# All transfers of the samples issued by SyncE, matrices over h and k and the inverse's scratch in 128 rows, a plan that knows of eight transfers under way

## The chip, the core and the metric

The kernel runs on one core of one Trainium2 chip. A core has five engines that run their own instruction streams: TensorE (PE; its weight loads are listed apart as PEld), VectorE (DVE), ScalarE (ACT), GpSimd (POOL) and SyncE (SP). Transfers between DRAM and the on-chip memory are carried by 16 DMA engines; they are issued by SP or by ACT, each with a queue of its own. The metric is the device time of one execution in microseconds; shorter is better.

## The reference, cut to what matters

The input x has 32 images of 56 x 56 pixels and 96 channels. Two layers follow one another.

```python
# layer 0: a convolution block whose weights are mixed per image (E = 4 experts, M = 384)
pooled = mean(x, axis=(1, 2)); rw = sigmoid(pooled @ Wr + br)
Wk = einsum('be,ecm->bcm', rw, Wpw)
h = relu(bn1(einsum('bhwc,bcm->bhwm', x, Wk) + rw @ bpw))
h = relu(bn2(sum over e of (depthwise 3x3 of h with Wdw[e] + bdw[e]) * rw[:, e]))
Wk2 = einsum('be,emf->bmf', rw, Wpwl)
x = bn3(einsum('bhwm,bmf->bhwf', h, Wk2) + rw @ bpwl) + x

# layer 1a: tokens t [32, 3136, 96]; a product in the frequency domain, hidden width 192
h = relu(bn1(layernorm(t) @ w1.T))
X = fft(h, axis=1, norm='ortho')
xr = relu(X.real * rd - X.imag * id + rb); xi = relu(X.imag * rd + X.real * id + ib)
t = t + bn2(ifft(xr + 1j * xi, axis=1, norm='ortho').real @ w2.T)

# layer 1b: a feed-forward net whose operands are rounded to an 8-bit and a 16-bit float
t = t + qlinear(relu(qlinear(layernorm(t), W1, b1)), W2, b2)
```

The Fourier transform over 3136 tokens is split in two steps of 56 (3136 = 56 x 56): one along the image's h with a twiddle factor, one along w. The values before the transform are real, so 29 of 56 frequencies suffice (K1).

## The kernel before, in words

**An image at a time, but in one long plan.** `record(b)` writes down the operations of image b: for each its engine, a duration, a due time, what it reads, writes and which buffers it takes. Nothing is issued then. When all 32 images are recorded, `Plan.order()` plays the operations through with the durations it was given, engine by engine, and the order in which they start there is the order in which the instructions are issued (lines 1445 to 1448). Each engine then runs its own instructions strictly in that order. The due times come from `WANT` (offsets from the image's start at multiples of `period`) and from `NUDGE`, one number for each operation of an image, added to its due time (line 233). An operation of DVE or ACT that reads the PSUM banks is due `HURRY` earlier. An operation that has been ready for `PATIENCE` and lacks a buffer holds that buffer back from operations behind it (line 319).

**Transfers in the plan.** `move` (line 225) adds a transfer: an operation of SP, or of ACT with `by="ACT"`, that takes 0.35 or 0.475 us to issue; its data then arrive one transfer after the other, `DMA_LAG` after the issue at the earliest. `slack` (2.0 for most, 0.0 for those by ACT) is added to the time at which its data are counted as ready to send.

**Layer 0** is done for two halves of the image and three chunks of 128 of the 384 channels. Chunk 2 goes by `by_vector` (line 845), where DVE makes eight of nine taps of the depthwise filter. Chunks 0 and 1 go by `by_tensor` (line 904), where TensorE does the filter. There the expand matmuls (32 columns at a time, `ps<-x,wk 97*32`) leave pixels of four parities on four groups of 32 partitions; ACT copies them with a ReLU into `hg`, and four transfers spread them into `hp` so that channel group and parity are on the right partitions ("hp<-h" in the profile, line 941). TensorE convolves, ACT brings the result back into `hp`, and four transfers send it into `hid` ("h<-hp", line 978), from where `project` multiplies it into 96 channels. Both sets of four are issued by ACT: 2 halves x 2 chunks x 8 = 32 transfers an image.

**Layer 1a** is done in four strips of 14 columns of the image. `da` (line 1101) is the matrix along h for the strip, loaded from the DRAM scratch `dad` by two transfers of 56 rows each, one for each parity of w. The result goes through the DRAM scratch `gd` ("gd<-g", "g<-gd"), the frequencies are handled in seven groups, and the inverse's first step goes into the DRAM scratch `yd` ("yd<-y", line 1302). For the inverse's second step `yt` (from `yd`) and `dd` (the matrix over k, from the input `dftd`) are loaded for each strip; both have 116 rows, and each is loaded by one transfer of 112 rows and one of 4 (lines 1319 and 1326). `back_h` multiplies them.

**Layer 1b** follows for the strip on TensorE, ACT, DVE and POOL, and the result leaves by SP ("out_dram<-xs").

**Preparation.** Before the images, constants are loaded and combined. `pack` (line 521) brings the matrix along h into the two halves' layout and writes it to `dad`, of 112 rows.

Of the kernel before, what the change touches and what calls it, by code (L numbers as in the profile page):

```python
# [19 lines left out]
C = 96  # L20
# [134 lines left out]

DMA_LAG = 1.9


def packets(n, size):
# [7 lines left out]
WANT = dict(period=120.0, expand=0.0, vector=1.4, forward=10.7, forward_step=27.0, freq=172.2,  # L167
            freq_step=7.0, tail=259.2, tail_step=26.5, x=17.0, mix=33.5, project=33.0)

HURRY = 160.2  # L170

PATIENCE = 0.2
# [4 lines left out]
    12.4, 22.1, 10.5, 25.3, -46.9, 6.9, 9.8, -31.8, 17.7, 22.8, 16.9, -1.6, 25.2, -10.2, -27.6, 5.2, 14.6, -15.7,  # L177
    49.7, 34.1, 32, 57.2, 7.6, -16.6, -19.8, -22.6, -16.6, -11.1, -12.4, -12.2, -15.8, 11.6, 14.1, 13.8, 29.2, 15,
    3.4, -6.4, 6.1, -32.1, -24.8, 30.6, 37.1, 14.9, 25.7, 0.1, -8.5, -2.7, -25.9, -54.5, -54.2, 12.1, 29.2, -31.5,
    14.5, 5.3, 2.9, -1, -2.8, -4.9, 18.2, 26.7, 23, 3.3, 18.2, -4.4, 7.7, 4.5, -11.1, -7.5, -11, -1.7,  # L180
    -46.2, -17.3, -2.1, -23.9, 13.1, -8.7, 14.3, -11, 14.7, 25.3, 3.9, 5.6, 0.7, 2.5, -16.3, -15, -2.1, 7.5,
    -10.9, 9.9, -11.5, -28.5, 0, 1.6, 10.1, -10.4, 11, 16.7, 28.4, 0.7, -37.6, -9.4, -13.9, -7.1, -28.9, -6.9,
    -14.8, -27.7, 0.8, 28.3, 20.5, 10.5, -1.8, 10.5, 18.1, -29.6, -37.7, -27.2, 25.5, 4.7, 14.8, 25.1, 12.5, 10.2,
    20.6, -6.3, -50.8, -56.5, 10, 27.5, 8.1, -9.8, -9.2, 20.2, -4.7, -2.5, 35.8, 15, 38.3, -1.6, 5.8, 15.5,
    11.1, -0.9, -2.7, -3.3, -3.5, -23.1, -10.1, -46.5, -6.8, 5.4, -14.9, -8.6, -6.9, -32.5, -11.2, 10.7, 14.5, 13.5,
    20.5, 16.8, -3.3, 10.4, 31.9, 2.9, 17, 4.1, -3.4, -17.3, -2.5, 12.5, 20.1, -8.8, 14.4, 11.1, 14.5, 1.9,
    -1.6, 19.4, 0.8, 10.7, -33.2, -38.3, -2.5, -4.1, -3, 11.9, -5.4, -47.3, 26.7, 14, -1, -16, -0.6, -29.3,
    8.7, 1.3, 11.8, -0.5, 0.5, 9.4, -37.9, -30.9, 1.7, -9.6, -1.5, 7.4, 9.9, -38.9, 21, 10.9, 10.2, -1.8,
    -12.2, -40.3, 13, 29.1, -5.1, 5.8, -4.9, -13.3, -42.9, -49.7, -55.1, -20.4, -40.3, -2.6, -34.5, -54.1, 4.9, -23.7,
    -7.1, -18.3, -6, -40.4, 19.5, 14.4, -3.4, -2.3, 13.7, 6.4, -29, -29.1, -17.7, -24.8, -15.7, -2.8, -2.9, -26.4,  # L190
    12.5, 9.1, -7.2, -12.2, -23, -49.8, 2.1, -10.6, -58.6, -12.9, -26.5, -2.4, -15.2, 14.5, -37.7, -10, -37.3, -0.7,
    -10.9, 4, -24.3, -12.2, 1.7, 5.4, -28.2, -2.2, -37, -17.2, -12.4, -6.4, 20.8, -17.2, -39, 42, -50.4, 5.6,
    3.6, -3.9, 29.1, 5.9, -27.6, 9.4, -25.9, 5, 13.4, 5.9, -10.2, 11.5, 28.1, 20.5, -24.7, 5.4, -47.4, 7.1,
    4.1, -0.7, 11.5, 2, -73.8, 33.8, -38.8, -14.4, 3.6, 2.1, 23.7, 20.1, -18.2, -7.7, -41.5, 24.5, -1.4, 2.2,
    -5.1, 1.1, 18.4, 19.6, -9.6, -15.1, -41.3, -12.8, 0.4, -1.1, 48.3, 4.2, -51.5, 58.4, -59.6, 3.4, -3.1, 0.8,
    16.9, 25.7, -5.4, 5, -24.6, 11.5, 10.5, 1.9, 0.7, 7.3, 9.9, 17.5, -1.7, 13.1, -14.5, 2, -7.2, -3.5,
    28.9, -11.4, -53.9, 49.3, -50.2, -1.7, -1, -1, 11, 8.9, -35, -5.1, -46.9, -12.2, -2.5, -0.3, -21.2, -2.3,
    -5.5, -6.3, -26.8, 9.4, -33.7, 9.5, 1.9, 2.6, 5.1, -2.1, -53.9, 51.5, -45.3, -2.6, 0, -9.3, 9.9, -4,
    -31.7, 3.9, -37.4, -7.8, 2.4, 11.4, -7.7, -4, 2, 14.8, -33.6, -3.7, -23.7, 6.6, 1.7, 0.9, 28.6, -8.6,
    -44.6, 46.4, -32.1, -9.4, 18.6, 0.4, -0.7, 8.6, -30, 2.9, -24.1, -6.2, -4.7, 14.1, -14, 4.8, 11.2, 9.1,  # L200
    -48.8, 3.6, -31.8, 12.2, -7.4, -10.5, 35.7, -7.9, -25, 41, -12.1, 1.4, 25.3, 3.5, 27.6, 2.1, 30.6, -6,
    3.2, 1.4, 22.5, 45.6, 14.3, -40, -4.7, 24.9, -15.7, 78.9, -13.2, 34.9, 1.3, 44.8, -2, 26.3, -29.2, 74.9,
    -3.3, 17.2, 8.9, 0.3, 1.1, 18.7, 25.2, 11.9, 28.4, 18.6, 8.5, 13.8, 8.9, 40.3, 2.5, -1, 2.9, 1.6,
    28.9, -11.8, -69.5, -27, 6.7, -13, 76.4, -12.9, 15.7, -4, 88.9, -6, 4.1, -21.6, 57.2, -1.6, 3.2, 0.6,
    3, -16.1, -4.9, 15.1, -11.5, 16.1, 5.5, 1.6, 9, 4.3, 28.2, 4.6, 27.2, 4.9, 3.5, 16.5, -10.6, -30.1,
    -22.7, 22.8, -15, 63.3, -5.2, 29.1, -11.2, 62.8, -40, -2.3, -15.3, 62.2, -13.6, -48, -20.5, -22, -39.8, -14,
    -12.2, -13, -2.6, 5.9, 33.1, 8.9, 9.1, 43.2, -29.5, 9.5, -8, -9.9, 17.9, -14.4, -50.3, -36.4, 39.3, 18.7,
    78.8, -12.6, 25.5, -2.1, 81.9, 3.6, 10.8, -8.5, 76.4, 8.5, 37.6, 21.8, 17, 24.2, 6, 21.7,
# [4 lines left out]
class Plan:  # L213
# [49 lines left out]
    def order(self):  # L263
# [5 lines left out]
        until = {"DVE": 0.0, "POOL": 0.0}  # L269
        waiting = []  # L270
        done = []

        def push(t, kind, x):
            nonlocal n
            n += 1
            heapq.heappush(events, (t, n, kind, x))
# [5 lines left out]
        def start(op, now):  # L282
            for b in op.takes:
                b.got = b.ring.take(b.n)
            begin = now
            if op.port:
                if op.eng == "POOL" and until["DVE"] > now:
                    waiting.append(op)
                    free["POOL"] = float("inf")
                    done.append(op)  # L290
                    return
                begin = max(now, until["POOL"])
                until[op.eng] = begin + op.dur
            op.end = begin + op.dur
            free[op.eng] = op.end
            done.append(op)
            if op.size:
                nonlocal moved
                moved = max(moved, op.end + DMA_LAG) + op.size
                push(moved, "end", op)  # L300
            else:
                push(op.end, "end", op)
# [73 lines left out]
def kernel(  # L376
# [97 lines left out]
    dad = dram.tile([PB, NQ, 2 * KR], F32, tag="dad", name="dad")  # L474

    with tc.tile_pool(name="prep", bufs=1) as pp:
        def temp(shape, name, dt=F32):
# [9 lines left out]
            par[:, :], ident[:, 0:PB].rearrange("z (p h) -> z p h", p=2), AX.X, ALU.add  # L487
# [29 lines left out]
        big = temp([PB, NQ // 2, PA], "big")  # L517
        small_a = temp([PB, NQ // 2, 2 * KR], "small_a")
        nc.vector.memset(small_a, 0.0)

        def pack(i):
            nc.scalar.dma_start(big, dfta[:, i * (NQ // 2) : (i + 1) * (NQ // 2)])
            v = big.rearrange("z q (k p r) -> z q k p r", p=2, r=2)
            to = small_a.rearrange("z q (r k) -> z q k r", r=2)[:, :, 0:K1]
            for q in range(NQ // 2):
                nc.vector.tensor_scalar_mul(to[:, q], v[:, q, :, 0], par[:PB, 0:1])
                nc.vector.scalar_tensor_tensor(to[:, q], v[:, q, :, 1], par[:PB, 1:2], to[:, q], ALU.mult, ALU.add)
            nc.sync.dma_start(dad[:, i * (NQ // 2) : (i + 1) * (NQ // 2)], small_a)
# [137 lines left out]
        for i in range(2):  # L666
            pack(i)
        nc.vector.tensor_copy(fw1, f1, saturate=False)
# [26 lines left out]
    r_dd = places(2, [PA, SQ, PB], F32, "dd")  # L695
# [9 lines left out]
    r_yt = places(2, [PA, SQ, C], F32, "yt")  # L705
# [11 lines left out]
    r_yd = ring(2, [PA, NQ, C], F32, "yd", dram)  # L717
# [25 lines left out]
    def record(b):  # L743
# [160 lines left out]
        def by_tensor(h, c, due, hid):  # L904
# [36 lines left out]
            for r in range(4):  # L941
                move(
                    packets(32, 6960), due - WANT["expand"] + 2,
                    lambda r=r: se.dma_start(
                        hp.ap[32 * r : 32 * r + 32].rearrange("p g n -> p (g n)"), hg.ap[r::4, :]
                    ),
                    by="ACT", slack=0.0,
# [30 lines left out]
            for q in range(4):  # L978
                move(
                    packets(32, 6272), due + 3,  # L980
                    lambda q=q: se.dma_start(
# [3 lines left out]
                    by="ACT", slack=0.0,  # L985
# [98 lines left out]
        for st in range(NS):  # L1084
# [17 lines left out]
            for p in range(2):  # L1102
                move(
                    packets(S, 1792), due - 5,
                    lambda p=p, st=st, da=da: sy.dma_start(
                        da.ap[XW * p : XW * p + S], dad[S * p : S * p + S, st * SQ : st * SQ + SQ, :]
                    ),
                    writes=[(da, p)], takes=[da] if p == 0 else [],
                )
            for q0, nq in ((0, 4), (4, 3)):  # L1110
# [27 lines left out]
                def along_h(q0=q0, nq=nq, ps=ps, ha=ha, da=da):  # L1138
# [11 lines left out]
                    "PE", 0.78, due + 3, along_h, reads=[(ha, 0), (da, 0), (da, 1)], writes=[(ps, 0)], takes=[ps, g],  # L1150
# [160 lines left out]
        for st in range(NS):  # L1311
# [7 lines left out]
            for a, z in ((0, PB), (PB, PA)):  # L1319
                move(  # L1320
                    packets(z - a, 2688), due - 6,
                    lambda a=a, z=z, st=st, yt=yt: sy.dma_start(yt.ap[a:z], yd.ap[a:z, st * SQ : st * SQ + SQ, :]),
                    reads=[(yd, i) for i in range(len(GROUPS))], writes=[(yt, a)], takes=[yt] if a == 0 else [],
                )
            dd = Buf(r_dd)
            for a, z in ((0, PB), (PB, PA)):
                move(
                    packets(z - a, 3136), due - 6,
                    lambda a=a, z=z, st=st, dd=dd: sy.dma_start(dd.ap[a:z], dftd[a:z, st * SQ : st * SQ + SQ, :]),
                    writes=[(dd, a)], takes=[dd] if a == 0 else [],  # L1330
                )
            ps = Buf(banks, 2)

            def back_h(ps=ps, yt=yt, dd=dd):
                for q in range(SQ):
                    te.matmul(
                        ps.pair[:C, 128 * q : 128 * q + 128].rearrange("c (p h) -> c p h", h=64)[:, :, 0:S],
                        yt.ap[:, q, :],
                        dd.ap[:, q, :].rearrange("c (p h) -> c p h", h=S),
# [223 lines left out]
```

## Time and profile before

| what | value |
|---|---|
| median of the runs | 4509.07 us (3 runs, 4507.47 to 4515.27) |
| the profiled execution's own time | 4500.26 us |
| its span, first to last instruction | 4498.5 us |
| mean granted TensorE clock | 0.955 |
| PE, DVE, ACT, POOL busy | 4036.7, 3514.9, 2518.6, 1484.5 us |
| transfers issued by ACT in the images | 512 hp<-h, 512 h<-hp |
| moved by all queues | 719.51 MB, 160 GB/s |

How to read the profile: times are microseconds unless marked ns. A group of instructions is named by line, engine, operation and out<-in in the program's own names, buffer numbers left out; after the bar stand its busy time, the mean of one, and the idle time of its engine just before such instructions, with what ended that idle time. Nearly every operation is issued through one helper, so its line is L370 everywhere and groups are told apart by tiles. A row of waits reads: who waited, for whom, the total, how many times, the longest. "SPq" and "ACTq" are the instructions that issue transfers; they are not counted as busy, nor is the time in which an engine stands before one. A wait for several semaphores is put down to the one that came last. A granted clock of 0.50 means that TensorE ran at half speed.

### The profile page before, as it was taken

Reading aid. Unit: us, or ns where it says so; the run is one execution under the profiler, and the core shown is the slowest. Engines: PE = TensorE matmul, PEld = TensorE weight load, DVE = VectorE, ACT = ScalarE, POOL = GpSimd, SP = SyncE. Lnnn points to the kernel's source line nnn. Section 1 sums busy time; section 2 is a strip of 40 time slices with the busy share of each in tenths; the row PEclk is TensorE's granted clock in tenths of the full one; section 3 lists DMA queues with packets and bytes.
Section 4 is the critical chain, followed back from the end, with each engine's and each line's share of the span. In section 5 each row is a group of like instructions: output and inputs, shape, how many; then the busy total and the mean of one; then the engine's idle time right before and its main releaser. Section 6 shows DMA issues by size and latency. Waiting matters only on the chain. (4 is left out here: it accounts for less than half of the span.)

```text
span 4498.5 us, 114325 instructions
## 1 busy us (share of the span) xinstructions
PE 4036.7 (90%) x44802; PEld 2547.7 (57%) x44802; DVE 3514.9 (78%) x9663; ACT 2518.6 (56%) x4982; POOL 1484.5 (33%) x1361
## 2 busy tenths in 40 slices
PE   2999999999999999999999999999999999989896
PEld 1455555556555555555565655565555556555564
DVE  5677878888877787877878778888878888877765
ACT  2455655565665555655566655565655565665453
POOL 1123333333333333333333333333333333333333
PEclk9999999999999999999999999999999999999987
DMA  4866677676677676676666676766677676677652
GB/s 100 158 149 161 153 184 173 164 173 159 161 164 173 161 163 157 156 181 161 162 157 156 160 182 169 169 168 158 161 183 172 164 169 160 156 171 167 154 140 71
DMA packets 436660, 719.51 MB, mean 160 GB/s; under 512 B 160954, under 2 KB 294522, under 8 KB 436122
## 3 DMA queue, kind: packets, MB, share of 16 engines
q1 hardware_dynamic: 382176, 492.72, 43.2%
q10 hardware_dynamic: 53946, 219.49, 23.6%
q8 instruction: 354, 5.80, 0.6%
q14 instruction: 184, 1.51, 0.1%
HBM read 286.14 MB, written 209.06 MB: 110 GB/s over the span
## 5 line engine op out<-in xcount | busy, mean ns | idle before, releaser
L370 DVE SCALAR_TENSOR_TENSOR h<-h,small,h 128x784 f32<-128x784 f32 x1024 | 1094.7, 1072 | 89.1 <-ACT h L370 64.8
L370 POOL CAST h<-h 128x784 fp8e5<-128x784 f16 x384 | 454.3, 1194 | 1184.4 <-DVE h L370 1184.4
L370 PE MATMUL ps<-x,wk 97*32 97x435 f32 (+2 forms) x4608 | 715.2, 600 | 125.0 <-ACT h L370 86.2
L370 ACT ACTIVATE h<-ps 128x435 f32<-128x435 f32 (+2 forms) x768 | 394.2, 531 | 304.1 <-PE ps L370 231.4
L370 PE MATMUL ps<-hp,wg 32*32 32x392 f32 x16384 | 503.8, 511 | 23.6 <-issue 19.4
L370 PE MATMUL ps<-dftb_s,g 112*128 112x112 f32 (+1 forms) x3776 | 424.0, 281 | 69.0 <-DVE tmpa L370 33.6
L370 PEld LDWEIGHTS ps<-x,wk 97*32 97x32 f32 (+1 forms) x4608 | 197.4, 121 | 453.7 <-ACT h L370 218.4
L370 ACT ACTIVATE hp<-ps,small 128x392 f32<-128x392 f32 x512 | 262.9, 589 | 308.9 <-PE ps L370 202.8
L370 POOL TENSOR_TENSOR ln<-ln,mhalf 120x7 f32<-120x7 f32 (+1 forms) x256 | 420.6, 1643 | 21.3
L370 PEld LDWEIGHTS ps<-dftb_s,g 112*128 112x128 f32 (+1 forms) x3776 | 335.0, 165 | 162.0 <-DVE tmpa L370 51.9
L370 DVE SCALAR_TENSOR_TENSOR ha<-ps,ln,nshift 120x192 f32<-120x192 f32 x896 | 308.6, 409 | 143.8 <-PE ps L370 135.0
L370 ACT ACTIVATE h<-h 128x784 f32<-128x784 f32 x128 | 109.6, 856 | 554.8 <-DVE h L370 233.2
L370 PE MATMUL ps<-h,wk 32*96 32x392 f32 x4096 | 413.7, 540 | 3.7 <-DMA h<-hp 3.6
L370 PEld LDWEIGHTS ps<-hp,wg 32*32 32x32 f32 x16384 | 286.7, 104 | 181.9 <-issue 93.1
L370 DVE BATCH_NORM_STATS2 ln<-ps 120x6 f32<-120x96 f32 (+1 forms) x1792 | 318.4, 248 | 72.5 <-PE ps L370 72.2
L370 PE MATMUL ps<-w1c,x 96*120 96x192 f32 x1792 | 345.9, 337 | 3.8 <-ACT hp L370 2.4
L370 ACT CAST h<-ps 128x784 f16<-128x784 f32 x384 | 299.2, 814 | 85.3 <-PE ps L370 62.0
L370 DVE TENSOR_SCALAR nt<-ps,ln 112x96 fp8e5<-112x96 f32 x896 | 267.0, 368 | 97.8 <-POOL ln L370 96.7
L370 PEld LDWEIGHTS ps<-h,wk 32*96 32x96 f32 x4096 | 212.1, 176 | 229.1 <-issue 108.2
L370 POOL TENSOR_TENSOR xs<-xs,y 96x784 f32<-96x784 f32 x128 | 214.0, 1671 | 353.5 <-ACT tmpb L370 199.1
L370 PEld LDWEIGHTS ps<-w1c,x 96*120 96x120 f32 x1792 | 290.4, 185 | 59.2 <-issue 25.1
L370 POOL COPY park<-x 96x784 f32<-96x784 f32 x128 | 109.9, 859 | 600.2 <-DVE x L370 574.2
(171 smaller groups left out, 7083.9 us busy)
## 6 DMA issues: line engine op xcount, KB each, us to landing
hp<-h ACTq DMA_DIRECT2D x512, 217.5 KB
h<-hp ACTq DMA_DIRECT2D x512, 196.0 KB
gd<-g SPq DMA_DIRECT2D x384, 192.0 KB
g<-gd SPq DMA_DIRECT2D x192, 336.0 KB
dd<-in_dftd_dram SPq DMA_DIRECT2D x128, 343.0 KB
xd<-park SPq DMA_DIRECT2D x128, 294.0 KB
xs<-xd SPq DMA_DIRECT2D x128, 294.0 KB
yt<-yd SPq DMA_DIRECT2D x128, 294.0 KB
```

What stands on the lines that cost most here:

```text
L370: return self.tc.keep_in_program_order(method(*args, **kwargs))
```

## The change

**Who issues.** The eight transfers of `by_tensor` (four hp<-h, four h<-hp) are issued by SP instead of ACT, at the same due times and with the same slack of 0.0. ACT issues none in the images any more.

**128 rows.** `dad` gets 128 rows, with each parity's 56 rows at rows 0 and 64 and zeros between, so `da` comes by one transfer of 128 rows instead of two of 56. `yd` gets 128 rows, and a copy of `dftd` with 128 rows, `ddd`, is made in DRAM during the preparation, with the rows past 116 zero; `yt` and `dd` come by one transfer of 128 rows instead of two of 112 and 4. `back_h` still multiplies the first 116 rows. That is twelve transfers an image less. In the preparation `big` and `small_a` are cleared by POOL, `big` is loaded by two transfers a half, and `rows_of_128` issues five transfers on ACT.

**The plan.** `order()` now keeps eight lanes: a transfer begins when the first of them is free again, and gives one back when its data have arrived. `NUDGE` has new values throughout (562 numbers for 574, one for each operation of an image), `HURRY` goes from 160.2 to 115.8, `PATIENCE` from 0.2 to 0.0 and `period` from 120.0 to 120.2. The order of the instructions on every engine follows from these.

```diff
+LANES = 8
...
-HURRY = 160.2
-PATIENCE = 0.2
+HURRY = 115.8
+PATIENCE = 0.0
...
         until = {"DVE": 0.0, "POOL": 0.0}
+        lanes = [0.0] * LANES
...
+            if op.size:
+                begin = max(now, lanes.pop(0))
             op.end = begin + op.dur
...
                 moved = max(moved, op.end + DMA_LAG) + op.size
+                lanes.append(moved + LAG["SP"])
...
-    dad = dram.tile([PB, NQ, 2 * KR], F32, tag="dad", name="dad")
+    dad = dram.tile([128, NQ, 2 * KR], F32, tag="dad", name="dad")
+    ddd = dram.tile([128, NQ, PB], F32, tag="ddd", name="ddd")
+    r_yd = ring(2, [128, NQ, C], F32, "yd", dram)
...
-        nc.vector.memset(small_a, 0.0)
+        nc.gpsimd.memset(big, 0.0)
+        nc.gpsimd.memset(small_a, 0.0)
...
-            nc.scalar.dma_start(big, dfta[:, i * (NQ // 2) : (i + 1) * (NQ // 2)])
+            part = slice(i * (NQ // 2), (i + 1) * (NQ // 2))
+            for p in range(2):
+                nc.scalar.dma_start(big[XW * p : XW * p + S], dfta[S * p : S * p + S, part])
...
+        def rows_of_128():
+            zero = temp([128 - PA, NQ, PB], "zero")
+            nc.gpsimd.memset(zero, 0.0)
+            nc.scalar.dma_start(ddd[0:PB], dftd[0:PB])
+            nc.scalar.dma_start(ddd[PB:PA], dftd[PB:PA])
+            nc.scalar.dma_start(ddd[PA:128], zero)
+            for t in r_yd.places:
+                nc.scalar.dma_start(t[PA:128], zero[:, :, 0:C])
...
-                    lambda r=r: se.dma_start(
+                    lambda r=r: sy.dma_start(
                         hp.ap[32 * r : 32 * r + 32].rearrange("p g n -> p (g n)"), hg.ap[r::4, :]
                     ),
-                    by="ACT", slack=0.0,
+                    slack=0.0,
...
-                    lambda q=q: se.dma_start(
+                    lambda q=q: sy.dma_start(
...
-                    by="ACT", slack=0.0,
+                    slack=0.0,
...
-            for p in range(2):
-                move(
-                    packets(S, 1792), due - 5,
-                    lambda p=p, st=st, da=da: sy.dma_start(
-                        da.ap[XW * p : XW * p + S], dad[S * p : S * p + S, st * SQ : st * SQ + SQ, :]
-                    ),
-                    writes=[(da, p)], takes=[da] if p == 0 else [],
-                )
+            move(
+                packets(128, 1792), due - 5,
+                lambda st=st, da=da: sy.dma_start(da.ap, dad[:, st * SQ : st * SQ + SQ, :]),
+                writes=[(da, 0)], takes=[da],
+            )
...
-            for a, z in ((0, PB), (PB, PA)):
-                move(
-                    packets(z - a, 3136), due - 6,
-                    lambda a=a, z=z, st=st, dd=dd: sy.dma_start(dd.ap[a:z], dftd[a:z, st * SQ : st * SQ + SQ, :]),
-                    writes=[(dd, a)], takes=[dd] if a == 0 else [],
-                )
+            move(
+                packets(128, 3136), due - 6,
+                lambda st=st, dd=dd: sy.dma_start(dd.ap, ddd[:, st * SQ : st * SQ + SQ, :]),
+                writes=[(dd, 0)], takes=[dd],
+            )
```

`yt` changes in the same way as `dd`, and reads `yd`.

## The prediction, made before the result was known

> **What bounds the kernel.** I read the first part of the page, then the steady stretch by window, then who ended TensorE's idle time there, then ACT's and SP's timelines at the gaps.
>
> ```profile
> PE 4036.7 (90%) x44802; PEld 2547.7 (57%) x44802; DVE 3514.9 (78%) x9663; ACT 2518.6 (56%) x4982; POOL 1484.5 (33%) x1361
> q1 hardware_dynamic: 382176, 492.72, 43.2%
> q10 hardware_dynamic: 53946, 219.49, 23.6%
> ```
>
> TensorE is the bound: 90% busy, nothing else over 78%. q1 is SP's queue, q10 ACT's; together they keep the 16 DMA engines two thirds busy. One image recurs in the trace every 135.07 us: from 337.7 to 4254.6 us are 29 images. The windows of that stretch, of one undisturbed image, and of three pieces of it (columns: window, its length, busy time of PE, PEld, DVE, ACT, POOL, granted clock, DMA share, GB/s):
>
> ```profile
> 3040.80:3047.60 6.80, 6.46 (x33) 2.13 (x37) 4.57 (x11) 3.42 (x7) 4.45 (x3) 0.50 1.01 234
> 3047.60:3173.90 126.30, 117.24 (x1371) 75.80 (x1363) 104.17 (x288) 75.25 (x150) 42.46 (x40) 1.00 0.68 165
> 3173.90:3180.70 6.80, 6.72 (x33) 2.12 (x37) 4.53 (x11) 3.16 (x7) 4.14 (x3) 0.50 1.00 214
> 337.70:4254.60 3916.90, 3615.10 (x40602) 2281.83 (x40606) 3141.60 (x8613) 2275.06 (x4494) 1347.92 (x1218) 0.97 0.70 165
> 3041.10:3174.00 132.90, 123.72 (x1404) 77.95 (x1404) 108.55 (x298) 78.48 (x156) 46.72 (x43) 0.98 0.70 168
> ```
>
> In 3916.9 us TensorE idles 301.8. It also runs at half clock for 6.8 us once an image, at one place (3040.8, 3173.9). The trace's clock marks give 269.7 us of half clock in this stretch, 41 pieces; half of it, 135 us, is lost. Idle time and lost clock, 437 us, are all that faster surroundings can give back here: 15 us an image. TensorE's waits in the same stretch (total, times, longest):
>
> ```profile
> PE ps L370 <- ACT h L370: 114.9, 62, 4.2
> PE ps L370 <- DVE tmpa L370: 74.4, 108, 1.2
> PE ps L370 <- issue: 29.3, 20, 4.1
> PE ps L370 <- ACT g L370: 27.4, 23, 2.6
> PE ps L370 <- ACT n L370: 26.4, 29, 0.9
> PE ps L370 <- ACT hp L370: 7.5, 10, 2.4
> ```
>
> ACT ends 176 us of it. Of "ACT h", 86.2 us stand before one form, the 97x32 expand matmuls, in gaps of 2.3 to 4.2 us, one an image. The timelines at one of them, ACT's then TensorE's:
>
> ```profile
> 3034.49 1.14 ACTq L370 DMA_DIRECT2D hp<-h  x2
> 3038.64 1.12 ACTq L370 DMA_DIRECT2D hp<-h  x2
> 3039.81 0.86 ACT L370 ACTIVATE h<-h 128x784 f32<-128x784 f32 x1 [3.19 <-DVE ln L370]
> 3041.14 1.68 PE L370 MATMUL ps<-x,wk 97*32 97x435 f32 x8 [2.44 <-ACT h L370]
> ```
>
> ACT finishes its Cast at 3036.6, stands until 3038.6 before it may issue two more transfers, spends 1.12 us on them, and only then reads the banks that TensorE waits for. The half clock begins in this gap. What ACT stood for is plainer at 2196, ACT's rows and then TensorE's:
>
> ```profile
> 2196.42 6.55 ACTq L370 DMA_DIRECT2D h<-hp  x4
> 2203.09 1.54 ACT L370 ACTIVATE hp<-ps,small 128x392 f32<-128x392 f32 x3 [5.92 <-DMA dd<-in_dftd_dram]
> 2206.12 1.46 PE L370 MATMUL ps<-hp,wg 32*32 32x392 f32 x2 [4.09 <-issue]
> ```
>
> h and hp have nothing to do with dd. The trace shows why: all 3477 transfers of both queues carry one of eight completion semaphores, 434 or 435 each, and a transfer waits for the one that had its semaphore before. So ACT stands for SP's transfers.
>
> **The change, part by part.** Per image, 75 transfers are issued by SP and 32 by ACT, 107 over eight semaphores. The three merges (da, yt, dd) take 12 from SP and the move adds 32: 95, all SP's.
>
> *ACT freed.* 32 issues at a median of 0.475 to 0.49 us are 15.5 us an image, and the waits before them (324 us in the run by the trace's gaps, 10 an image) go too. ACT is 56% busy, so this counts only where TensorE waits behind it. The recurring gap is that: **-86 us**. The irregular gaps of the kind at 2206 ("issue" at the hp,wg form 12.7 here, "ACT g" 27.4, "ACT hp" 7.5; 48 us) I take for half: **-24 us**, since g is copied beside the issues but also late by its own inputs.
>
> *The clock.* The Trainium skill, TensorE: Matmul & The Clock Gate, "Why this matters for your kernels", warns of idle gaps over about 3 us and of one idle window. By that rule a 2.4 us gap costs 2.4 us and no clock, and this term is nothing. The row says otherwise: half clock begins at gaps of 2.44 and 2.52 us, while the 1.2 us gaps before DVE tmpa show none. The measurement decides: 29 pieces belong to the recurring gap, 6.6 us each, halved, 96 us; all 41 are 135. In the other order of work another gap can be long enough, so I take half of 135: **-67 us**. By the rule the sum below would be 67 us slower.
>
> *SP lengthened.* Before: gd 16 at 0.60, da 8 at 0.54, 51 others at about 0.33, 31 us an image. After: 16 at 0.60, 4 at 0.54, 43 at 0.33, 32 at 0.48, about 41 us of 135. There is room, but SP works in order, and its waits are long:
>
> ```profile
> SPq L370 <- ACT y L370: 762.6, 199, 8.8
> SPq L370 <- POOL park L370: 526.4, 111, 11.1
> ```
>
> That is 3.8 and 4.7 us a time, for yd<-y and xd<-park. A set of hp<-h or h<-hp behind one is late, and behind it the conv or projection matmuls. Now TensorE waits almost never for them; from the last landing of a set of hp<-h to its conv are 1.9 us in the lowest quarter of the 128 sets, 4.7 in the middle. On the other side the four issues of a set, spread over 4.7 us on ACT (median), can go in 2. The cost lies between 0 and 256 us (each of 256 sets late by 1 us); I take a quarter of the sets late by 1 us, the lowest quarter: **+64 us**. The Trainium skill, DMA: Bandwidth & Descriptors, "Issuing engines are not separate DMA queues", calls the sequencer time saved "usually small relative to the DMA itself"; by it the ACT term is nothing and this one stays, 4564. The row of 2.0 + 1.12 us inside a 2.44 us gap speaks against it here.
>
> *More rows, fewer transfers.* 128 rows for 112 or 116 add 28 KB to da, 31.5 to yt, 36.8 to dd a strip, 12.3 MB on 719.5: DMA share 0.70 becomes 0.71. The wait for this stays under the transfers' slack (yt's landing is 7 us ahead of its matmul in the lowest quarter); nothing. If it were not hidden, 1.7% of 3000 busy DMA us would be 51.
>
> *Preparation.* One memset moves from DVE to POOL and two are new; x's 1920 columns took 1.65 us there, so big's 1624 and zero's 3136 take about 4 us together, early, while POOL idles until 82 us. ACT gets seven more issues before image 0: two for the second halves of big, five for ddd and the pads. The 1.4 MB copy of dftd into ddd is 9 us at 160 GB/s. SP's first dd load, at 74 us, must wait for it, and behind that stand image 1's first x loads and wk2's pieces. Between 0 and 20; **+5 us**.
>
> *Order.* NUDGE, HURRY, PATIENCE and the lane count give every engine another order. The trace of before can't show it; its bound is the 437 us above on one side and as much again on the other. I leave the middle at nothing and widen the range.
>
> **Sum**, against the profiled execution's own 4500.3 us (span 4498.5): -86 -24 -67 +64 +5 = -108, 4392. The median of the runs shown, 4509.1, is 9 us above that execution, so **4401**; the measurement's own spread makes about 0.2% (9 us) the least that can be told from no change.
>
> **Rivals.**
> (a) ACT freed entirely and nothing in return: all of 86 + 48 + 135 = 269 less, 4231 and 9: 4240. For it: TensorE's own work at full clock is (3615 - 135) / 29 = 120 us an image, and no other engine is near that. Against: DVE at 78% ends 74 us of waits that the change does not touch, and SP's price.
> (b) SP's queue holds the sets (slower). Place: hp<-h and h<-hp behind yd<-y and xd<-park. If 4 us are added before every set, the slack above leaves a mean of 1 us late; 256 sets are 256 us, such stalls keep the half clock, and only 110 of the gain stays: 4500 - 110 + 256 + 5, and 9: 4660. It decides from about 0.7 us a set (177 / 256). For it: SP's waits; against it: twelve fewer transfers an image over the eight semaphores, and room on SP.
> (c) The stall changes its owner: the recurring gap goes, another of over 2 us comes with its half clock, and the irregular gaps stay; 4500 - 86 + 64 + 5, and 9: 4492, 0.4% faster, with "same" inside its spread.
> (d) The move hides: the gaps follow from data, not from issue, no change, 4509. Against it is the row at 2196.
>
> **Chances.** Sum as above 0.50 (own range 4320 to 4475), (a) 0.15, (c) 0.12, (d) 0.03, (b) 0.20. Faster: 0.50 + 0.15 + two thirds of (c) = 0.73; same 0.04 of (c) and 0.02 of (d): 0.06; slower 0.21. The range leaves out two fifths of (a), 0.06, and two thirds of (b), 0.13: 4230 to 4590.
>
> **What would show it.** Right: no DMA issue on ACT after the preparation; the 97x32 expand's "ACT h" idle near nothing; one period without a half-clock piece, granted clock over 0.98; period near 131.5 us; SP's waits naming eight-semaphore predecessors. Wrong: TensorE idle ended by DMA h<-hp or DMA hp<-h over 100 us; a new gap over 2 us an image; DVE in ACT's place; a granted clock under 0.95.

## The result, and the profile after

| | before | changed |
|---|---|---|
| median of the runs | 4512.2 us | 4438.6 us (4425.8 to 4444.4) |
| ratio, 95% interval | | 0.9833 (0.9809 to 0.9858) |
| profiled execution, span | 4498.5 us | 4442.5 us |
| granted clock | 0.955 | 0.962 |

1.7% faster, 74 us between the medians and 56 us between the two profiled spans (the profiled execution of the changed kernel, 4444.4 us, is the longest of its runs). The forecast was 4401 us, 108 us less than before. Its sign was right and its size near, but its parts were not what they were taken for.

The head of the page of the changed kernel, with its transfer queues:

```profile
PE 4003.5 (90%) x44802; PEld 2605.1 (59%) x44802; DVE 3535.3 (80%) x9669; ACT 2507.0 (56%) x4975; POOL 1432.2 (32%) x1364
q1 hardware_dynamic: 433920, 722.30, 70.4%
q10 hardware_dynamic: 5618, 4.49, 0.4%
```

(The helper that issues stands at line 376 here, 371 in e5 and 400 in e6.) ACT's queue, q10, is left with the preparation. TensorE is still the bound, at the same 90%. Windows of the changed kernel (columns as before): the 29 images of the steady stretch, one undisturbed image, one disturbed one.

```profile
333.60:4214.50 3880.90, 3599.98 (x40769) 2346.82 (x40769) 3167.98 (x8633) 2271.33 (x4507) 1296.05 (x1222) 0.97 0.74 170
3148.90:3277.90 129.00, 119.88 (x1401) 79.01 (x1401) 109.24 (x297) 78.03 (x156) 44.46 (x42) 1.00 0.75 176
2881.80:3019.40 137.60, 127.22 (x1400) 82.76 (x1400) 108.29 (x297) 78.13 (x156) 44.67 (x42) 0.94 0.71 165
```

The stretch is 36 us shorter, although it holds 167 matmuls more than that of before (40769 for 40602). TensorE's idle time in it fell by 21 us and its half-clock time by 41 (by 44 in the stretch of the table further below); half of that is lost time, so the 29 images gained some 41 of the 56 us, and the rest lies ahead of them and behind. The single images say more than the mean. An undisturbed image fell from 132.9 to 129.0 us and keeps the full clock, which over 29 images would be 113 us. But only 11 of the 29 images take under 131 us, and 5 take over 137 (counted from one first matmul with dftb_s in it to the next); such images take the larger part back. TensorE's waits in the stretch, and two of its groups over the whole run:

```profile
PE ps L376 <- ACT h L376: 93.3, 114, 1.3
PE ps L376 <- DVE ha L376: 38.1, 30, 1.3
PE ps L376 <- DMA g<-gd: 35.9, 27, 3.2
PE ps L376 <- issue: 30.4, 25, 2.9
```

```profile
L376 PE MATMUL ps<-dftb_s,g 112*128 112x112 f32 x1856 | 274.8, 292 | 60.4 <-DMA g<-gd 36.1 <-DVE tmpa L376 11.4 <-ACT zb L376 9.3
...
L376 PE MATMUL ps<-x,wk 97*32 97x435 f32 x4096 | 456.2, 576 | 0.0
```

The 86.2 us before the 97x32 expand matmuls are gone, to the last tenth. In their place stand shorter waits for ACT at other forms (114 of them, 0.8 us on average, none over 1.3), 1.3 us an image for DVE, and a wait that the kernel before did not have: up to 3.2 us for the loads g<-gd. This last one makes the most disturbed images: such gaps of 1.7 us or more stand in 10 of the 29. Of the 225 us of half clock in the changed kernel's 29 images, 85 follow gaps for g<-gd, 58 follow seven "issue" gaps before the hp,wg form, and 48 follow seven of the gaps for DVE (each half-clock piece put down to the longest gap in the 3.5 us before it). SP's timeline of the image above, with the TensorE row that waited:

```profile
2982.59 1.23 SPq L376 DMA_DIRECT2D gd<-g  x2
2983.91 0.55 SPq L376 DMA_DIRECT2D da<-dad  x1
2991.01 2.43 SPq L376 DMA_DIRECT2D hp<-h  x4
2993.54 0.53 SPq L376 DMA_DIRECT2D dd<-ddd  x1
2994.28 0.47 SPq L376 DMA_DIRECT2D hp<-h  x1
2994.80 1.11 SPq L376 DMA_DIRECT2D g<-gd  x2
2995.95 2.70 SPq L376 DMA_DIRECT2D hp<-h  x3
```

```profile
3006.03 0.74 PE L376 MATMUL ps<-dftb_s,g 112*128 112x112 f32 x2 [3.25 <-DMA g<-gd]
```

SP stands 6.5 us, from 2984.5 to 2991.0, until ACT has the data of a set of hp<-h. The two g<-gd are behind it in the order. When they go out, five transfers of 217 KB and one of 392 KB are ahead of them and three more follow, so they land 11 us later, and TensorE stands 3.25 us.

### The profile page after: what moved, and what is told of

It is laid out like the page before. It is cut to its first block, busy times and chain, and to the rows that moved or that the text cites. A ratio compares the mean times of both kernels' runs of the same rounds, so it can differ in the third digit from the quotient of the medians.

```text
span 4442.5 us, 114026 instructions
## 1 busy us (share of the span) xinstructions
PE 4003.5 (90%) x44802; PEld 2605.1 (59%) x44802; DVE 3535.3 (80%) x9669; ACT 2507.0 (56%) x4975; POOL 1432.2 (32%) x1364
## 4 chain that ended last, share of the span: by engine, by line
PE 52%; DVE 18%; ACT 10%; DMA 9%; issue 4%; POOL 4%; SPq 1%; POOLq 0%; ACTq 0%; DVEq 0%
PE ps L376 52%; DMA g<-gd 6%; POOL ln L376 4%; DVE za L376 3%; ACT h L376 3%; DVE h L376 3%; DVE ha L376 3%; DVE ln L376 2%; DVE tmpa L376 2%; ACT tmpa L376 2%; DVE zb L376 2%; SPq L376 1%; DMA yt<-yd 1%; ACT za L376 1%; DVE tmpb L376 1%
## 5 line engine op out<-in xcount | busy, mean ns | idle before, releaser
L376 DVE SCALAR_TENSOR_TENSOR h<-h,small,h 128x784 f32<-128x784 f32 x1024 | 1064.2, 1051 | 48.5 <-ACT h L376 29.3
L376 POOL CAST h<-h 128x784 fp8e5<-128x784 f16 x384 | 413.9, 1082 | 989.7 <-DVE h L376 986.5
L376 PE MATMUL ps<-x,wk 97*32 97x435 f32 (+2 forms) x4608 | 680.9, 575 | 14.7 <-ACT h L376 11.1
L376 PE MATMUL ps<-hp,wg 32*32 32x392 f32 x16384 | 518.9, 516 | 36.8 <-issue 25.4
L376 PEld LDWEIGHTS ps<-dftb_s,g 112*128 112x128 f32 (+1 forms) x3776 | 356.3, 171 | 167.6 <-issue 100.7
L376 POOL TENSOR_TENSOR ln<-ln,mhalf 120x7 f32<-120x7 f32 (+1 forms) x256 | 447.6, 1748 | 21.3
L376 PE MATMUL ps<-h,wk 32*96 32x392 f32 x4096 | 359.8, 492 | 0.0
L376 DVE TENSOR_SCALAR h<-h,fb 128x784 f16<-128x784 f16 x384 | 240.8, 633 | 99.7 <-ACT h L376 99.4
L376 ACT COPY g<-ps 128x768 f32<-128x768 f32 x256 | 206.1, 807 | 183.1 <-PE ps L376 176.5
```

The lines of the kernel that those rows point to most:

```text
L376: return self.tc.keep_in_program_order(method(*args, **kwargs))
```

## The experiments

The change has three parts that can be had apart: who issues, the rows and number of the transfers, and the order of the work. The order of a kernel can be held while the issuer changes: the plan is made as it was, and only the engine that issues is another. Each result below is a median, then the ratio to the kernel before, measured beside it, with its 95% interval. Gains read from medians and from ratios differ by up to 15 us, so where it matters both are given.

**e2: the issuer alone.** The order of before on all other engines.

```diff
# before.py, both sets; the plan still counts them as ACT's
-                    lambda r=r: se.dma_start(
+                    lambda r=r: sy.dma_start(
...
-                    lambda q=q: se.dma_start(
+                    lambda q=q: sy.dma_start(
```

> The kernel before with its own order on every other engine, only the 1024 transfers issued by SP instead of ACT, at the same places. Issuer theory: the idle time before the 97x32 expand matmuls (86 us) falls under 20, the half-clock piece of each image goes with it, and the time is 4350 to 4460 us. Order theory: SP, with 107 transfers an image and an order not laid out for it, holds the sets back, and the time is 4512 us or more.

Measured: 4424.7 us, 0.9847 (0.9820 to 0.9873). The issuer alone is worth 84 us by the medians and 1.5%, 69 us, by the ratio. Of its reasons one half held. Two groups of TensorE, in the kernel before and then in e2:

```profile
L370 PE MATMUL ps<-x,wk 97*32 97x435 f32 x4096 | 504.5, 605 | 86.2 <-ACT h L370 86.2
...
L370 PE MATMUL ps<-dftb_s,g 112*128 112x112 f32 x1856 | 270.8, 287 | 54.5 <-ACT n L370 28.2 <-DVE tmpa L370 21.2 <-ACT y L370 0.9
```

```profile
L370 PE MATMUL ps<-x,wk 97*32 97x435 f32 x4096 | 475.4, 575 | 10.9 <-ACT h L370 9.3 <-issue 1.6
...
L370 PE MATMUL ps<-dftb_s,g 112*128 112x112 f32 x1856 | 305.1, 312 | 91.8 <-ACT n L370 76.9 <-DVE tmpa L370 5.6 <-DMA g<-gd 2.4
```

The idle time before the expand fell from 86.2 to 10.9 us. But before another form, the first matmuls of the frequency groups, it rose from 54.5 to 91.8, with ACT n in it from 28.2 to 76.9. And the half clock stayed: 266 us of the 29 images, 270 before. A gap of 2.6 us an image now stands some 15 us further on in the image and has taken the half clock with it; in idle time it is half of what went, since the two groups together fell from 140.7 to 102.7 us. SP did not hold the sets back, as the rival wanted: TensorE waited 3.9 us in all for hp<-h before the hp,wg form.

**e3: the rows alone.** ACT issues, the order of before; each of da, yt and dd in one transfer of 128 rows, the second one's place in the order left empty.

```diff
# before.py with the changed preparation, dad, ddd and yd in 128 rows
-                    lambda p=p, st=st, da=da: sy.dma_start(
-                        da.ap[XW * p : XW * p + S], dad[S * p : S * p + S, st * SQ : st * SQ + SQ, :]
+                    lambda p=p, st=st, da=da: None if p else sy.dma_start(
+                        da.ap, dad[:, st * SQ : st * SQ + SQ, :]
# yt and dd likewise
```

> The kernel before with its own order and issuers, only da, yt and dd in one transfer of 128 rows each (twelve transfers an image fewer over the eight semaphores; the second transfers' places in the order stay, empty). My prediction: nothing, within 10 us of 4512. Semaphore theory (what ACT stands for is the eighth transfer back, so fewer transfers mean shorter waits): 20 to 80 us faster, with the time that ACT stands before its issues (324 us) down by a fifth or more. Traffic theory (12 MB more): up to 50 us slower.

Measured: 4448.9 us, 0.9884 (0.9847 to 0.9921). That is 60 us by the medians, 52 by the ratio, for a part that was put at nothing. Which of its reasons it is, e8 tells.

**e8: 128 rows, in two transfers each.** As many transfers as before, with the rows of e3, evenly cut (da 64 and 64, yt and dd 112 and 16).

```diff
# e3
-                    lambda p=p, st=st, da=da: None if p else sy.dma_start(
-                        da.ap, dad[:, st * SQ : st * SQ + SQ, :]
+                    lambda p=p, st=st, da=da: sy.dma_start(
+                        da.ap[XW * p : XW * p + XW], dad[XW * p : XW * p + XW, st * SQ : st * SQ + SQ, :]
# yt and dd: rows 0 to 112 and 112 to 128
```

> The kernel before with 128 rows as in e3, but each of da, yt and dd in two transfers again (da 64 and 64 rows, yt and dd 112 and 16): as many transfers as before, in 128 rows. Count theory (e3's gain of 60 us came from twelve transfers fewer over eight semaphores): no gain, 4490 to 4530 us. Spread theory (it came from even rows over the 16 DMA engines, or from the preparation): as e3, 4430 to 4465 us.

Measured: 4530.9 us, 1.0059 (1.0037 to 1.0080), slower than before by 23 us. So the 128 rows cost a little (by their bytes or by the longer preparation; that was not tried apart), and the number of transfers is what gained: between e8 and e3, which move the same bytes by the same issuers in the same order, lie 82 us (79 by the ratios) for twelve transfers an image. The group of the recurring gap, in e8 and then in e3:

```profile
L370 PE MATMUL ps<-x,wk 97*32 97x435 f32 x4096 | 507.4, 608 | 101.9 <-ACT h L370 101.8
```

```profile
L370 PE MATMUL ps<-x,wk 97*32 97x435 f32 x4096 | 474.3, 574 | 23.6 <-ACT h L370 23.5
```

The semaphore updates in the traces name what ACT stood for at this gap. In the kernel before, at 28 of the 29 gaps, it was the third transfer of a set of hp<-h, which carries the same completion semaphore as the first transfer of the same set; it goes out 21 ns after that semaphore's last update, when the first has landed. The eight semaphores are given out in turn over both queues, and around these two SP issues da, dd and g<-gd in two transfers each. In e8 the same pair stands at 27 of 29 gaps. In e3, with da and dd in one transfer each, the third transfer has another semaphore: ten gaps over 0.8 us are left, and nine of them are for a gd<-g. So it is the pairing that gained here; that any other twelve transfers fewer would do the same was not tried.

ACT's standing time before issues as a whole fell by less than expected: 303 us in the 29 images became 273, a tenth instead of a fifth. What counted was the one place where TensorE was behind it, and part of that came back: the group before dftb_s,g rose from 54.5 to 78.3 us, as in e2.

**e4: both, in the order of before.** e3 with e2's edit: all of the change but the new order.

> The kernel before with its own order, the transfers issued by SP and the 128 rows: all of the change but the new order. Issuer theory: within 30 us of the changed kernel's 4439, on either side, so that the new order is worth little. Order theory: over 4500, so that the new order is worth 60 us or more.

Measured: 4411.1 us, 0.9810 (0.9788 to 0.9832), and once more, beside the changed kernel:

> e4 once more (the order of before, SP issues, 128 rows), beside the changed kernel on one chip, to settle the sign of the new order: 0.979 to 0.983 of the kernel before. If the new order costs, the changed kernel lies above this by 20 to 40 us; if it is worth nothing, the two lie within 10 us.

> The changed kernel beside e4: 0.983 to 0.987 of the kernel before, above e4 by 20 to 40 us if the new order costs.

e4 4417.1 us, 0.9809 (0.9783 to 0.9834); the changed kernel 4444.0 us, 0.9865 (0.9832 to 0.9897). The intervals just touch, and side by side the changed kernel lies 27 us above. Its other two ratios (0.9833, and 0.9868 below) lie 10 and 26 us above e4's first. So the new order, as it was, did not gain; it cost about 27 us where both ran side by side. And the gains do not add: by the medians 84 us for the issuer, 60 for the rows and 98 for both, since both removed the same gap (before the expand stand 10.9, 23.6 and 9.7 us).

> The changed kernel once more, beside the others on one chip: 4425 to 4445 us, 0.981 to 0.986 of the kernel before. With e4's 0.979 to 0.983 it tells whether the new order is worth less than the old one.

Measured: 4449.1 us, 0.9868 (0.9830 to 0.9906).

**e1: the new order, issued by ACT again.**

```diff
# after.py, both sets
-                    lambda r=r: sy.dma_start(
+                    lambda r=r: se.dma_start(
...
-                    lambda q=q: sy.dma_start(
+                    lambda q=q: se.dma_start(
```

> The changed kernel with its own order and 128 rows, but the 1024 transfers hp<-h and h<-hp issued by ACT again, at the same places of the order. Issuer theory (ACT standing before and in its issues is what TensorE waited for): the gain is lost and more, since this order was laid out for a free ACT: over 4490 us, with TensorE's waits for ACT up by over 60 us. Order theory (the new order is what gained): within 15 us of the changed kernel, 4425 to 4455 us.

Measured: 4517.4 us (4483 to 4574), 1.0008 (0.9982 to 1.0034). The whole gain is gone: against the ratios of the changed kernel, 0.9833 to 0.9868, the issuer is worth 63 to 79 us in the new order too. TensorE's waits for ACT in the 29 images rose from 116 to 228 us. This profile is of one of the shortest executions, 4484.6 us. It has less half clock than the changed kernel (164 us for 225), and before the expand only 12.0 us: here ACT is late at many places (ACT h 134 us, ACT g 52), not at one.

**e5: the gap that moved.** It stands in e4 as it did in e2. Its group in e4, and one instance of it, ACT's rows and then TensorE's:

```profile
L370 PE MATMUL ps<-dftb_s,g 112*128 112x112 f32 x1856 | 304.3, 311 | 98.9 <-ACT n L370 78.3 <-DVE tmpa L370 10.8 <-DMA g<-gd 3.0
...
3785.81 0.86 ACT L370 ACTIVATE h<-h 128x784 f32<-128x784 f32 x1 [9.82 <-DVE h L370]
3786.57 0.80 ACT L370 ACTIVATE n<-ps 96x784 fp8e5<-96x784 f32 x1
...
3787.43 0.77 PE L370 MATMUL ps<-dftb_s,g 112*128 112x112 f32 x2 [2.57 <-ACT n L370]
```

ACT stands for DVE's taps ahead of its ReLU, and n, whose banks TensorE waits for, is behind.

```diff
# e4, after the plan is made
+    for one, two in zip(acts, acts[1:]):
+        if one.tag == "last" and two.tag == "n":
+            i, k = done.index(one), done.index(two)
+            if not any(op in one.after for op in done[i : k + 1]):
+                done.insert(k, done.pop(i))
```

> e4 (order of before, SP issues, 128 rows) with one thing moved: in each image where ACT's last ReLU of the vector path stands directly ahead of the feed-forward net's cast n, it goes behind it (30 places). In e4 TensorE's recurring gap is 2.57 us before the dftb_s,g matmuls, ended by ACT n, and ACT had stood 9.8 us for DVE at that ReLU. Moved-stall theory (the gap that SP's issue took away came back here, with its half clock): the gap falls to 0.9 us, TensorE's waits for ACT n from 85 to under 40 us, half-clock time of the 29 images from 280 to under 170 us, and the time from 4411 to 4290 to 4350 us. Rival (TensorE then waits for DVE, which is the true limit): the gap turns up before another form, and the time stays within 20 us of 4411.

Measured: 4394.5 us, 0.9753 (0.9709 to 0.9796), 17 us below e4's first median (some 25 by the ratios); the theory wanted 60 or more. The group in e5:

```profile
L371 PE MATMUL ps<-dftb_s,g 112*128 112x112 f32 x1856 | 286.0, 298 | 95.1 <-DVE tmpa L371 57.5 <-ACT n L371 28.2 <-DMA g<-gd 2.7
```

ACT n went back from 78.3 us in e4 to 28.2, as it should. The idle time stayed, 95.1 for 98.9: now DVE's tmpa, in line behind its own taps, is the last to give a bank. Half clock did fall, from 280 to 181 us. The rival was right that DVE is the limit behind ACT, though the gap stayed before the same form and did not turn up before another.

**e6: the loads ahead of the sets.** The changed kernel, with the order of SP alone put right at 62 places.

```diff
# after.py, after the plan is made; need[op]: the last operation that op has to follow
+        for other in reversed(sps[max(0, k - 10) : k]):
+            if at[other] <= need[op]:
+                break
+            if other.tag == "hp":
+                ahead = other
+        if ahead is not None:
+            moves.append((op, ahead))
...
+    for op, ahead in moves:
+        done.remove(op)
+        done.insert(done.index(ahead), op)
```

> The changed kernel; only in SP's order the loads g<-gd go ahead of the set of hp<-h that stood before them (62 places), where nothing that they need lies between. Queue theory (the price of issuing all by SP is that hp<-h, for which SP stands 3 to 7 us, holds the loads that are ready): TensorE's waits for DMA g<-gd (36 us) go under 5, with a part of the half clock, and the time is 4370 to 4420 us. Burst theory (1.7 MB of hp<-h saturate the DMA engines, whatever the order in the queue): the waits turn to DMA hp<-h and the time stays within 20 us of 4439.

Measured: 4346.1 us (4332.7 to 4354.4), 0.9641 (0.9609 to 0.9673), beyond what was expected and the fastest of all kernels here. The group in e6:

```profile
L400 PE MATMUL ps<-dftb_s,g 112*128 112x112 f32 x1856 | 259.2, 281 | 31.6 <-DVE tmpa L400 18.8 <-ACT zb L400 9.3 <-ACT n L400 2.0
```

DMA g<-gd no longer stands in it, and TensorE does not wait for hp<-h in its place, as the burst theory wanted (7.6 us before hp,wg, for 5.3). Against the changed kernel on the same chip (4449.1) these are 103 us, and the 29 images show where they came from (TensorE's idle time and half-clock time of each profiled execution, in us; counted here from one matmul with wr_s in it to the same one 29 images later, a stretch that begins some 80 us before that of the windows above; in the changed kernel and e6 it holds 100 matmuls fewer than in the other rows, some 0.5 us an image, so compare within one order):

| kernel | us an image | TensorE idle | at half clock |
|---|---|---|---|
| before | 134.9 | 299 | 270 |
| changed | 133.0 | 282 | 225 |
| e2, issuer | 132.0 | 226 | 266 |
| e3, rows | 133.6 | 259 | 287 |
| e4, both | 132.5 | 240 | 280 |
| e6 | 129.6 | 243 | 99 |

From the changed kernel to e6: 39 us less idle, and half of 126 us less half clock, 63: together 102. The clock is the larger part. Of the half clock, the 85 us behind gaps for g<-gd are gone, and the 58 behind "issue" gaps before hp,wg became 10; what those gaps waited for, no row names. The gaps for DVE stayed, with 68 us behind them for 48.

**e9: the same thing for ACT, everywhere.** e6, and each last ReLU of the vector path behind the next two ACT operations, if none of them needs it.

```diff
# e6, ACT's order
+        while k + 1 < len(done) and seen < 2:
+            k += 1
+            if done[k] in op.after:
+                break
+            if done[k].eng == "ACT":
+                seen += 1
+                to = k
```

> e6 (the changed kernel, loads g<-gd ahead of the sets of hp<-h) and in ACT's order each last ReLU of the vector path behind the next two ACT operations, where none of them needs it (128 places). ACT stands 467 us in 123 waits for DVE at these. Theory (what stands behind such a wait on ACT holds TensorE's banks): TensorE's waits for ACT h fall from 99 to under 60 us and the time from 4346 to 4290 to 4325. Rival (these waits cost nothing, since what stands behind has slack, and the projection then comes later): within 15 us of 4346, or slower.

Measured: 4463.4 us, 0.9910 (0.9883 to 0.9938), 117 us slower than e6. TensorE's waits for ACT h rose from 99 to 139 us, those for DVE tmpa from 19 to 63, and the half clock from 99 to 253 us. ACT's standing for DVE turned into standing for TensorE (ACT hp from 184 to 439 us). So what was put ahead of the ReLU was not ready either, and the ReLU came later. The rule of e6, first what is ready, was not what this edit did.

## Why the prediction was right, point by point

*ACT freed, -86 and -24.* Right in place, too high in size: 0.0 us are left before the expand and "ACT g" went from 27 to 6, but all waits for ACT fell by 60 us of the 110. What the sum left out is that other waits for ACT take their place: 93 us of short ones for ACT h instead of 29 (114.9 less 86.2). In the order of before (e2, e4) a gap of 2.6 us came back at ACT n. That is rival (c), the stall that changes its owner, with its half clock, but with a gain of 69 to 84 us where the rival gave 17. The reading that ACT stands for SP's transfers holds at 2196; at the recurring gap ACT stood for its own, the first transfer of the same set, and SP's issues only set which two share a semaphore.

*The clock, -67.* Failed in size: half of 44 us, -22. The row was read rightly against the rule that the prediction cites (a gap under 3 us does cost the clock). The term was still wrong, because the half clock goes with whatever gap is long enough, and each change made a new one: ACT n in e2 to e4, g<-gd and the "issue" gaps in the changed kernel. The half clock fell to 99 us only in e6, where none of these recurs.

*SP lengthened, +64.* Right in sign, wrong in mechanism, too small in size. I had looked for sets of hp<-h late behind yd<-y. It was the reverse: a set for which SP stands holds loads of another part of the image. TensorE's waits for hp<-h stayed at 5 us, and 36 us of waits for g<-gd came up. With the clock, e6 puts the price at 103 us, some 39 of waiting and 63 of clock.

*More rows, fewer transfers, nothing.* Wrong, -52 to -60 alone (e3). The working counted 107 and 95 transfers over eight semaphores and drew nothing from it. Beside SP's issue it is worth less, 14 to 17 us (e2 to e4).

*Order, nothing.* About +27 in the changed kernel against e4; the range held it. This and SP's price are one thing: with 62 loads put ahead (e6) the order, otherwise the same, is 65 us below e4.

*Preparation, +5.* The first image's matmul begins at 76.4 us for 76.9: nothing. (Two slips change nothing: the added rows are 12.6 MB, not 12.3, and 4564 leaves out the preparation and the 9 us to the median.)

So -108 stood against -74. The profile of the changed kernel has, in the forecast's own terms, ACT at -60 for -110, the clock at -22 for -67 and SP's loads at +36 for +64, with no term for the rows. (SP's price here is the waiting alone; its clock is in the clock's term.) The two gains were 95 us too high together and the price 28, so the errors partly cancelled. That the sum came within 34 us is in good part luck; what the prediction had right is that ACT's issuing held TensorE up before the expand, and that SP's queue would take a part back.

## What to carry to other kernels

When issues are moved to one queue, ask of each transfer what it has to stand for, and what that is ready stands behind it; a transfer that waits for a slow producer belongs behind the loads that are ready, and moving 62 of them was worth more (103 us) than freeing ACT (84 us). Where eight completion semaphores serve all transfers in turn, look up which two share one: two transfers of one set that did cost a gap in every image, and a change in their number that parted them was worth 82 us. A gap taken from a loop that is bound elsewhere tends to come back at the next place in line, so look for the whole chain of who is late before counting it, and count a gain in clock only when no long gap is left.

## What the runs showed of the hardware

How long a gap on TensorE must be before its clock is halved can be read from the 29 images of nine of these traces together (before, changed, e1 to e6, e8), by the gaps that began at full clock and had a half-clock piece begin within them or in the 3.5 us after:

| gap | followed by half clock |
|---|---|
| 0.8 to 1.1 us | 18 of 581 |
| 1.1 to 1.5 us | 30 of 312 |
| 1.5 to 2 us | 30 of 59 |
| 2 to 2.4 us | 32 of 44 |
| 2.4 to 3 us | 135 of 149 |
| over 3 us | 44 of 44 |

Gaps of 2.5 us cost twice: once as they are, and some 3.4 us in a half-clock piece of 6.8 us, the most frequent length.

The same traces show why the middle of the table is mixed. All half-clock pieces begin and end on a grid of 3.41 us that runs through the whole execution, so they last 3.4, 6.8 or 10.2 us, seldom longer. Whether a window of that grid turns slow goes with TensorE's idle time in the window just before it, counted here where that one was still at full clock:

| idle in the window before | turned slow |
|---|---|
| under 0.8 us | 1 of 8455 |
| 0.8 to 1.2 us | 22 of 609 |
| 1.2 to 1.4 us | 30 of 237 |
| 1.4 to 1.8 us | 56 of 86 |
| 1.8 to 2 us | 40 of 44 |
| 2 us or more | 140 of 140 |

So a gap counts by the part of it that falls into one window. The 56 gaps of 1.3 to 1.6 us before the n,fw form in the changed kernel and e6 show it: of the 39 that lie within one window, 16 are followed by half clock; of the 17 that a window's edge divides, one is, with 1.5 of its 1.6 us in one window. All this goes by gaps as they came; none were made on purpose.
